# Keys' differences in the slot of x, k, v and rows in one gap, and weighted sums copied by ScalarE in one step a block

## The chip, the cores and the metric

The kernel runs on one core of a Trainium2 chip. The metric is the device time of one execution in microseconds (us). A core has a matrix engine (TensorE, PE in the profile), a vector engine (VectorE, DVE), an activation engine (ScalarE, ACT), a general engine (GpSimd, POOL), and SyncE (SP), which here only issues DMA transfers. Each works through its own queue in order. Matmul results land in PSUM[...]; everything else is in SBUF.

## The reference, cut to what matters

Two layers over x of shape (2, 256, 64, 64), all in fp32. The change touches only the first, attention with 8 heads of 32 channels over 4096 positions:

```
q, k, v = split(w_qkv @ x[b])                    # per image b, 8 heads, 32 x 4096 each
scores  = q.T @ k / sqrt(32)                     # 4096 x 4096 a head
attn    = softmax(scores, axis=-1)
x       = w_proj @ (attn @ v) + x
```

The second layer is a non-local block: three 1x1 convolutions, two of them followed by 2x2 max pooling, a softmax over 1024 keys, one more convolution, batch normalization and a residual.

## The kernel before, in words

**Groups and blocks.** Four heads of 32 channels fill 128 partitions, so a group n (0 to 3) is one image and four heads; two groups belong to an image. In a group a block i (0 to 7) is 512 queries, and in a block a step j (0 to 31) is 128 keys. `attend` (from line 410) holds the loops; after an image's two groups come `project` and `non_local`.

**A step.** For two pairs of heads, heads 2 and 3 first, TensorE makes scores into a `ps_s` tile (`score`, line 439), ScalarE takes the exponential into `p` (line 574), and a step later TensorE multiplies `p` with v into a PSUM tile `w` (`weigh`, line 463), which VectorE adds to the block's sum `blk.num`, a part of `y` (line 473). The scores of step 0 stand in PSUM together with the negated row maxima ("rows"); later steps add to them the product of q with a *difference* of keys, so that `s` is turned from one set of 128 keys to the next. The differences are tiles made by GpSimd: `kd` and `last_kd` (a chunk of 512 keys with an odd number less the one before it), `mid_kd` (even less odd) and `turn_kd`.

**The sums of p** are GpSimd's: it adds the first half's `p` (line 491) in each step, and in each second step issues a DMA that accumulates the other half (line 497). `normalize` finishes a block during the next one: a DMA and an add (`whole`, lines 506 and 510), a sum over partitions on TensorE (`den`, line 518), a reciprocal that goes out and back by DMA on SP, and a multiply on GpSimd (line 549). It is advanced at j = 1 and 5 and from j = 8 on.

**The maxima.** Before a block's softmax its row maxima over all keys are needed. They are computed ahead: `maxima(n, i)` is a generator that `attend` advances twice a step, four steps (LEAD) ahead of the block boundary, so the maxima of a block are made during the block before, and end in the step of j = 27 to 28. Each advance issues the matmuls of two heads (`product`, line 286). For heads 0 and 1 each of 8 chunks of keys is *plain*: one matmul, and one maximum reduction on VectorE (line 298). For heads 2 and 3 two chunks make a *pair*: q times the difference of the chunks, whose positive part ScalarE writes to a tile `over` (line 305); then q times the first chunk, and VectorE's one instruction adds `over` and reduces (line 312). In the first block of groups 1 to 3 only chunks 0 to 3 of heads 2 and 3 are pairs and 4 to 7 are plain (line 352): their differences would be in `last_kd`, which the group before still reads then. Head 3 starts with one plain chunk and ends with another. At the end VectorE reduces `part` to `neg` (line 380), GpSimd splits it (lines 141 to 145), and `make_rows` lets TensorE transpose it and ScalarE store it as rows.

**PSUM.** The pool `ps_m` has four banks, taken in turn by the maxima's `ps`, by `w`, `den`, the rows' `pt`, and by the products of `make`. A matmul waits until the tile that had its bank four allocations earlier is read. In a step that order is heads 0 and 1, heads 2 and 3, `w`.

**The next group's k, v and q** are made meanwhile: `make` (line 168) loads 512 columns of x over SP into the one slot of tag "x", multiplies, and lets ScalarE copy the product out. `during(n, i)` (line 267) lists three such items a block; they run at j = 11, 19 and 27. k's chunk 3 also brings two differences into `kd`. `renew` (line 250) has GpSimd make the other differences over again at the end of a group and the start of the next, behind the add of that step.

**Order.** The engines' queues are planned in the program's order with each instruction's readiness; `issue_after(x)` puts instructions behind x on its engine. A tile's buffer is taken again when all that read it is done: two buffers of `over`, five double and six single buffers for `p`.

Of the kernel before, what the change touches and what calls it, by code (L numbers as in the profile page):

```python
# [9 lines left out]
F32 = mybir.dt.float32  # L10
# [12 lines left out]
P = 128  # L23
NC = C // P
NB = 512
NI = N // NB
NJ = N // P
# [8 lines left out]
def conv_attention(  # L36
# [13 lines left out]
    nc = tc.nc  # L50
# [5 lines left out]
    xs = ctx.enter_context(tc.tile_pool(name="xs", bufs=1))  # L56
    qkv = ctx.enter_context(tc.tile_pool(name="qkv", bufs=2))
    work = ctx.enter_context(tc.tile_pool(name="work", bufs=2))
# [9 lines left out]
    def scores(name):  # L68
        return ps_s.tile([P, 2, NB], F32, tag="s", name=name)

    def scratch(name):
        return ps_m.tile([P, NB], F32, tag="m", name=name)
# [3 lines left out]
    def single(name):  # L76
        return probs.tile([P, 2, NB], F32, tag="one", name=name, bufs=ONES)

    def double(name):
        return probs.tile([P, 2, 2, NB], F32, tag="two", name=name, bufs=TWOS)  # L80
# [53 lines left out]
    t = const.tile([P, NB // P, QH, D], BF16, name="terms")  # L134
# [29 lines left out]
    QUAD = [(b, qd) for b in range(B) for qd in range(QUADS)]  # L164
    q, k, v, kd = {}, {}, {}, {}
    held = {}
# [61 lines left out]
    last_kd = const.tile([P, NI // 4, NB], F32, name="last_kd")  # L228

    def differences(n, c, to):  # L230
        two = k[n][:, bass.ts(c, 2 * NB)]
        nc.gpsimd.tensor_sub(to, two[:, NB:], two[:, :NB])  # L232
# [31 lines left out]

    def during(n, i):
        if i < NI - 2:
            return [("q", n, i + 2), ("k", n + 1, i), ("v", n + 1, i)]
        if i == NI - 2:  # L270
            return [("k", n + 1, i), ("k", n + 1, i + 1), ("q", n + 1, 0)]
        return [("v", n + 1, i - 1), ("v", n + 1, i), ("q", n + 1, 1)]


    reduced, cut = None, None
# [3 lines left out]
    LEAST = -3.4028234663852886e38  # L279
    part = const.tile([P, NB // P, QH, NI], F32, name="part")  # L280
    nc.vector.memset(part, LEAST)

    def product(n, i, g, h, keys, ps=None):
        if ps is None:
            ps = scratch(f"ps_{n}_{i}_{g}_{h}")
        nc.tensor.matmul(  # L286
            ps,
            q[n, i][bass.ts(h, D), bass.ts(g, P)],
            keys[bass.ts(h, D), :],
            start=True,  # L290
            stop=True,
        )
        return ps

    def plain(n, i, g, h, j):
        nonlocal reduced
        ps = product(n, i, g, h, k[n][:, bass.ts(j, NB)])
        reduced = nc.vector.tensor_reduce(part[:, g, h, j : j + 1], ps, AX.X, ALU.max)  # L298

    def pair(n, i, g, h, jp):  # L300

        nonlocal cut
        ps = product(n, i, g, h, (kd[n] if jp < NI // 4 else last_kd)[:, jp % (NI // 4), :])
        over = work.tile([P, NB], F32, tag="over", name=f"over_{n}_{i}_{g}_{h}")
        cut = nc.scalar.activation(over, ps, AF.Relu)  # L305
        yield
        joint(product(n, i, g, h, k[n][:, bass.ts(2 * jp, NB)]), over, g, h, jp)
        yield

    def joint(ps, over, g, h, jp):  # L310
        nonlocal reduced
        reduced = nc.vector.tensor_tensor_reduce(  # L312
            out=ps,
            in0=ps,
            in1=over,
            scale=1.0,
            scalar=LEAST,
            op0=ALU.add,
            op1=ALU.max,
            accum_out=part[:, g, h, 2 * jp : 2 * jp + 1],  # L320
        )
# [26 lines left out]
    def of_head(n, i, h):  # L348

        chunks = 0 if h < 2 else NI // 2 if i == 0 and n > 0 else NI
        pairs = [(g, jp) for jp in range(chunks // 2) for g in range(G)]
        plains = [(g, j) for g in range(G) for j in range(chunks, NI)]
        if h == 3:
            if not plains:
                g, jp = pairs.pop()
                plains = [(g, 2 * jp), (g, 2 * jp + 1)]
            plain(n, i, plains[0][0], h, plains[0][1])
            plains = plains[1:]  # L360
            yield
        for x in pairs:
            yield from pair(n, i, x[0], h, x[1])
        for x in plains:
            plain(n, i, x[0], h, x[1])
            yield

    def maxima(n, i):
        if (n, i) == (0, 0):
            yield from first_block()  # L370
        else:
            heads = [of_head(n, i, h) for h in range(QH)]
            for step in range(G * NI):

                for two in (0, 1), ((2, 3) if step % 2 == 0 else (3, 2)):
                    for h in two:
                        next(heads[h])
                    yield
        neg = work.tile([P, NB // P, QH], F32, tag="neg", name=f"neg_{n}_{i}")
        nc.vector.tensor_reduce(neg, part, AX.X, ALU.max, negate=True)  # L380
        rows.append(negate(f"{n}_{i}", neg))
        if i == 0 and n > 0:
            nc.vector.memset(part[:, :, 2:, :], LEAST)


    rows = []
# [8 lines left out]
    def advance(steps, n=1):  # L395
        for _ in range(n):
            next(steps, None)
# [12 lines left out]
    def attend(b, y):  # L410
# [11 lines left out]
        def keys(j):  # L422

            return j % NI * (NB // P) + j // NI
# [23 lines left out]
        def subtract(s, pair, blk):  # L448
            for t in range(2):
                h = 2 * pair + t  # L450
                nc.tensor.matmul(
                    s[:, t, :],
                    ones_b[bass.ts(h, D), :],
                    rows[blk.rows][bass.ts(h, D), :],
                    start=True,
                    stop=False,
                )

        def weigh(blk, j, p):

            w = scratch(f"w_{blk.name}_{j}")
            for h in range(QH):
                nc.tensor.matmul(  # L463
                    w[bass.ts(h, D), :],
                    v[blk.n][:, keys(j), h, :],
                    p[h // 2][:, h % 2, :],
                    start=True,
                    stop=True,
                )
            if j == 0:  # L470
                nc.vector.tensor_copy(blk.num, w)
            else:
                nc.vector.tensor_add(blk.num, blk.num, w)  # L473

# [3 lines left out]
        added = None  # L478
# [73 lines left out]
        for qd in range(QUADS):  # L552
            for i in range(NI):
                blk = Block(qd, i)
                items = [x for x in during(blk.n, i) if x[1] < len(QUAD)]
                both = [None, None]
                for j in range(NJ):
                    if j % 2 == 0:
                        two = double(f"p_{blk.name}_{j}_1")
                    p = [single(f"p_{blk.name}_{j}_0"), two[:, j % 2]]  # L560
                    for pair in (1, 0):
                        if j == 0:
                            s = both[pair] = scores(f"s_{blk.name}_{j}_{pair}")
                            subtract(s, pair, blk)
                            advance(maxes)
                            score(s, pair, blk, j)
                        else:
                            s = both[pair]
                            score(s, pair, blk, j)
                            advance(maxes)  # L570
                        with ExitStack() as order:
                            if cut is not None:
                                order.enter_context(tc.issue_after(cut.ins))
                            nc.scalar.activation(p[pair], s, AF.Exp, scale=scale)  # L574
                    if waiting is not None:
                        weigh(*waiting)
                        if j == 0:
                            normal = normalize(waiting[0])
                    add(blk, j, p, two)
                    waiting = blk, j, p  # L580
                    if j in (1, 5) or j >= AFTER:
                        advance(normal)
                    if j % 2 == 0:
                        make_rows()
                        if i > 0 and blk.n + 1 < len(QUAD) or i == 0 and blk.n > 0:
                            with tc.issue_after(added.ins) if added else ExitStack():
                                renew(i, j, blk.n)
                    elif j % 8 == 3 and j > 8 and items:
                        advance(make(*items.pop(0)), 9)
        weigh(*waiting)  # L590
        return normalize(blk)

# [205 lines left out]
    LEAD = 4  # L798
# [4 lines left out]
    items = [("k", 0), ("q", 0), ("k", 1), ("v", 0), ("q", 1), ("v", 1)]  # L803
# [76 lines left out]
```

## Time and profile before

| what | value |
|---|---|
| median of 3 runs | 3923.11 us (3920.67 to 3923.43) |
| profiled execution | 3922.51 us, its span 3920.7 us |
| TensorE matmul busy | 3882.0 us, 99% |
| VectorE busy | 2940.4 us, 75% |
| ScalarE busy | 2654.9 us, 68% |
| GpSimd busy | 3051.9 us, 78% |
| clock granted to TensorE | 0.997 |

Busy time is the time in which at least one instruction of the engine was under way. Matmuls overlap, so 99% says that TensorE always has one in flight, not that it couldn't do more. Row groups give a line, engine, operation and tiles, then how many, the busy time, the mean duration of one in ns, the idle time before them and what ended it. A timeline row starts with its start and duration in us; "x2" means that two instructions of a kind that follow each other are drawn together. Attention takes the stretches of about 106 to 1741 us and 2034 to 3630 us; the rest is `project` and `non_local`.

### The profile page before, as it was taken

To read this page: it belongs to the slowest core of one execution; us is meant where nothing else is said; L and a number is where in the kernel's file an instruction comes from. 1 tells how busy PE (TensorE), PEld (TensorE's weight loads), DVE (VectorE), ACT (ScalarE), POOL (GpSimd) and SP (SyncE) were. 2 spreads that over 40 slices of the span, in tenths; PEclk is the share of its full clock that TensorE was granted. 3 is DMA by queue.
4 is the path that set the end of the run, shared out by engine and by line. 5 is a ranking of instruction groups with operands and counts; after the bars stand their busy time and mean duration, and the time that the engine had idled before them with its cause. 6 is when DMAs were issued, how large, how long until landed. Compare 5 with 4: busy or idle time off the path is not lost.

```text
span 3920.7 us, 69957 instructions
## 1 busy us (share of the span) xinstructions
PE 3882.0 (99%) x27452; PEld 1370.0 (35%) x27452; DVE 2940.4 (75%) x5483; ACT 2654.9 (68%) x3296; POOL 3051.9 (78%) x1926
## 2 busy tenths in 40 slices
PE   8999999999999999999999999999999999999998
PEld 3333333333333333343333333333433333332333
DVE  5888888888888888874458888888888888885444
ACT  4777777777777777741137777777677787787011
POOL 1788888889888888871448889898899999997043
PEclk9999999999999999999999999999999999999999
DMA  1688888887888888880018888888888888889100
GB/s 57 139 168 169 167 170 168 174 169 167 166 167 169 165 169 169 172 195 6 22 38 167 167 173 170 170 171 175 165 173 169 169 170 168 167 167 188 54 16 27
DMA packets 113931, 569.40 MB, mean 145 GB/s; under 512 B 20296, under 2 KB 22600, under 8 KB 52416
## 3 DMA queue, kind: packets, MB, share of 16 engines
q0 software_dynamic: 68832, 501.25, 63.7%
q1 hardware_dynamic: 44080, 62.88, 4.6%
q8 instruction: 215, 3.52, 0.4%
q14 instruction: 116, 0.95, 0.1%
q10 hardware_dynamic: 688, 0.79, 0.1%
HBM read 54.78 MB, written 8.88 MB: 16 GB/s over the span
## 4 chain that ended last, share of the span: by engine, by line
PE 53%; DVE 2%; DMA 1%; ACT 0%; issue 0%; POOL 0%; DVEq 0%; ACTq 0%; POOLq 0%
PE s L439 14%; PE w L463 13%; PE ps L286 11%; PE y L736 6%; PE g L661 1%; DVE r L750 1%; PE f L704 1%; PE proj L604 1%; PE f L770 1%; PE q L198 1%; PE den L518 1%; PE tp L645 0%; PE tp L641 0%; PE v L186 0%; PE k L198 0%; DMA x_res<-in_x_dram 0%
## 5 line engine op out<-in xcount | busy, mean ns | idle before, releaser
L491 POOL TENSOR_TENSOR p<-p,p 128x1024 f32<-128x1024 f32 x945 | 2350.5, 2487 | 363.4 <-ACT p L574 338.4
L574 ACT ACTIVATE p<-s 128x1024 f32<-128x1024 f32 x2048 | 2085.9, 1023 | 593.3 <-PE ps L286 528.5
L286 PE MATMUL ps<-k,q 32*128 32x512 f32 x6232 | 2016.1, 627 | 4.0 <-DVE part L298 1.7
L298 DVE TENSOR_REDUCE part<-ps 128x1 f32<-128x512 f32 x2136 | 1369.0, 685 | 541.8 <-PE ps L286 541.6
L463 PE MATMUL w<-p,v 128*32 128x512 f32 x8192 | 1091.9, 605 | 0.6 <-ACT p L574 0.6
L439 PE MATMUL s<-q,mid_kd 32*128 32x512 f32 x3072 | 767.4, 615 | 0.0
L473 DVE TENSOR_TENSOR y<-y,w 128x512 f32<-128x512 f32 x992 | 679.1, 685 | 47.1 <-PE w L463 46.4
L312 DVE CUSTOM_DVE_ANT_0 ps<-ps,over 128x512 f32<-128x512 f32 x980 | 674.5, 691 | 34.3 <-PE ps L286 31.2
L286 PEld LDWEIGHTS ps<-k,q 32*128 32x128 f32 x6232 | 628.1, 183 | 43.3 <-DVE part L298 8.9
L305 ACT ACTIVATE over<-ps 128x512 f32<-128x512 f32 x916 | 541.9, 592 | 18.0 <-PE ps L286 12.6
L286 PE MATMUL ps<-kd,q 32*128 32x512 f32 x1056 | 517.0, 594 | 0.7 <-POOL kd L232 0.7
L439 PE MATMUL s<-q,kd 32*128 32x512 f32 x2048 | 512.2, 615 | 0.4 <-ACT p L574 0.3
L439 PE MATMUL s<-q,last_kd 32*128 32x512 f32 x2048 | 509.8, 614 | 0.7 <-ACT p L574 0.7
L463 PEld LDWEIGHTS w<-p,v 128*32 128x32 f32 x8192 | 161.1, 108 | 804.6 <-DVE part L298 775.0
L286 PE MATMUL ps<-last_kd,q 32*128 32x512 f32 x904 | 438.0, 593 | 2.4 <-POOL last_kd L232 2.4
L439 PEld LDWEIGHTS s<-q,mid_kd 32*128 32x128 f32 x3072 | 262.0, 183 | 413.9 <-ACT over L305 225.6
L497 POOL DMA_DIRECT2D p<-p x448 | 392.2, 875 | 4.4 <-issue 3.1
L439 PEld LDWEIGHTS s<-q,kd 32*128 32x128 f32 x2048 | 177.1, 183 | 295.4 <-ACT over L305 171.9
L439 PEld LDWEIGHTS s<-q,last_kd 32*128 32x128 f32 x2048 | 176.7, 183 | 275.8 <-ACT over L305 162.7
L736 PE MATMUL y<-p,kv 128*128 128x512 f32 x512 | 240.0, 608 | 6.4 <-DVE r L750 6.4
L785 ACT ACTIVATE p<-f 128x1024 f32<-128x1024 f32 x64 | 65.5, 1024 | 248.5 <-PE f L770 219.2
L732 POOL TENSOR_TENSOR sums<-sums,p 128x512 f32<-128x512 f32 x96 | 121.3, 1264 | 113.7 <-ACT p L785 109.9
(113 smaller groups left out, 2686.7 us busy)
## 6 DMA issues: line engine op xcount, KB each, us to landing
p<-p POOLq DMA_DIRECT2D x478, 1024.0 KB, 7.5
x_k<-in_x_dram SPq DMA_DIRECT2D x32, 512.0 KB
x_q<-in_x_dram SPq DMA_DIRECT2D x30, 512.0 KB
x_res<-in_x_dram SPq DMA_DIRECT2D x16, 512.0 KB
out_dram<-z SPq DMA_DIRECT2D x16, 512.0 KB
r<-flat SPq DMA_DIRECT2D x120, 64.0 KB
x_v<-in_x_dram SPq DMA_DIRECT2D x6, 512.0 KB
wqk_sb<-in_wqk_dram ACTq DMA_DIRECT2D x1, 512.0 KB
```

Of the source, the lines that this page charges most:

```text
L286: nc.tensor.matmul(ps, q[n, i][bass.ts(h, D), bass.ts(g, P)], keys[bass.ts(h, D), :], start=True, stop=True,)
L298: reduced = nc.vector.tensor_reduce(part[:, g, h, j : j + 1], ps, AX.X, ALU.max)
L305: cut = nc.scalar.activation(over, ps, AF.Relu)
L312: reduced = nc.vector.tensor_tensor_reduce(out=ps, in0=ps, in1=over, scale=1.0, scalar=LEAST, op0=ALU.add, op1=ALU.max, accum_out=part[:, ...
L439: nc.tensor.matmul(s[:, t, :], kj[bass.ts(h, D), :], q[blk.n, blk.i][bass.ts(h, D), :], start=False, stop=True, skip_group_check=j > 0,)
L463: nc.tensor.matmul(w[bass.ts(h, D), :], v[blk.n][:, keys(j), h, :], p[h // 2][:, h % 2, :], start=True, stop=True,)
L473: nc.vector.tensor_add(blk.num, blk.num, w)
L491: added = nc.gpsimd.tensor_add(blk.sums[0], blk.sums[0], p[0])
L497: sent = nc.gpsimd.dma_start(out=blk.sums[n], in_=two, accum_op=ALU.add)
L574: nc.scalar.activation(p[pair], s, AF.Exp, scale=scale)
L732: nc.gpsimd.tensor_add(acc[i][NC], acc[i][NC], p[:, j, :])
L736: nc.tensor.matmul(acc[i][o], wg[:, 2 * t + j, bass.ts(o, P)], p[:, j, :], **edge)
```

## The change

Three things are edited.

1. *Differences in the slot of x.* At j = 8 of a group's last block, GpSimd writes the differences of the next group's chunks 5 less 4 and 7 less 6 into a tile `first_kd` in the one "x" slot (`before_all`). In the first block of groups 1 to 3 `pair` reads them in place of `last_kd`, so all 8 chunks of heads 2 and 3 are pairs there, and the memset that reset `part` after that block goes.
2. *Places of the items.* `during` now gives the items by step: q at j = 11, k and v together at j = 30, the step in which rows are made. In block 6 k and v of chunk 6 come at j = 11, q of the next group's block 0 at j = 19 and k and v of chunk 7 at j = 30; in block 7 only q of the next group's block 1, at j = 7.
3. *A copy by ScalarE.* In one step a block, j = 26 (its `w` is weighed in the pass of j = 27), ScalarE copies `w` to a tile of tag "over" in SBUF and VectorE adds that to `blk.num`. The very last block is left out.

```diff
+    first_kd = {}
+
     def during(n, i):
         if i < NI - 2:
-            return [("q", n, i + 2), ("k", n + 1, i), ("v", n + 1, i)]
+            return {11: [("q", n, i + 2)], NJ - 2: [("k", n + 1, i), ("v", n + 1, i)]}
         if i == NI - 2:
-            return [("k", n + 1, i), ("k", n + 1, i + 1), ("q", n + 1, 0)]
-        return [("v", n + 1, i - 1), ("v", n + 1, i), ("q", n + 1, 1)]
+            return {
+                11: [("k", n + 1, i), ("v", n + 1, i)],
+                19: [("q", n + 1, 0)],
+                NJ - 2: [("k", n + 1, i + 1), ("v", n + 1, i + 1)],
+            }
+        return {7: [("q", n + 1, 1)]}
+
+    def before_all(n):
+        held.clear()
+        first_kd[n] = xs.tile([P, NI // 4, NB], F32, tag="x", name=f"first_kd_{n}")
+        for c in range(2):
+            differences(n, NI // 4 + c, first_kd[n][:, c, :])
...
-        ps = product(n, i, g, h, (kd[n] if jp < NI // 4 else last_kd)[:, jp % (NI // 4), :])
+        those = kd[n] if jp < NI // 4 else first_kd[n] if i == 0 and n > 0 else last_kd
+        ps = product(n, i, g, h, those[:, jp % (NI // 4), :])
...
-        chunks = 0 if h < 2 else NI // 2 if i == 0 and n > 0 else NI
+        chunks = 0 if h < 2 else NI
...
-        if i == 0 and n > 0:
-            nc.vector.memset(part[:, :, 2:, :], LEAST)
...
+            elif j == NJ - LEAD - 2 and (blk.n, blk.i) != (len(QUAD) - 1, NI - 1):
+                t = work.tile([P, NB], F32, tag="over", name=f"w_{blk.name}")
+                nc.scalar.copy(t, w)
+                nc.vector.tensor_add(blk.num, blk.num, t)
             else:
                 nc.vector.tensor_add(blk.num, blk.num, w)
...
-                items = [x for x in during(blk.n, i) if x[1] < len(QUAD)]
+                items = during(blk.n, i)
...
-                    elif j % 8 == 3 and j > 8 and items:
-                        advance(make(*items.pop(0)), 9)
+                        if (i, j) == (NI - 1, 8) and blk.n + 1 < len(QUAD):
+                            with tc.issue_after(added.ins):
+                                before_all(blk.n + 1)
+                    for item in items.get(j, ()):
+                        if item[1] < len(QUAD):
+                            advance(make(*item), 9)
```

## The prediction

> **What bounds the kernel now.** I read the page first (busy times, the chain), then stretches of one block, then the timeline at two places. The page:
>
> ```profile
> PE 3882.0 (99%) x27452; PEld 1370.0 (35%) x27452; DVE 2940.4 (75%) x5483; ACT 2654.9 (68%) x3296; POOL 3051.9 (78%) x1926
> ...
> PE 53%; DVE 2%; DMA 1%; ACT 0%; issue 0%; POOL 0%; DVEq 0%; ACTq 0%; POOLq 0%
> ...
> L473 DVE TENSOR_TENSOR y<-y,w 128x512 f32<-128x512 f32 x992 | 679.1, 685 | 47.1 <-PE w L463 46.4
> ```
>
> TensorE carries the chain. A step is the time from one start of `w` (line 463) to the next: 2.96 us nearly everywhere, six waves of four matmuls (0.43 apart, 0.13 more at each change between row tiles and column tiles). Extra work shows as a longer step: q or k +1.91, v +1.98, `den` +0.86, rows +0.33, first scores +0.17. Three whole blocks (ordinary; last of four heads; ordinary of the last four heads):
>
> ```profile
> 614.40:716.20 101.80, 101.80 (x812) 34.92 (x808) 83.08 (x163) 80.01 (x101) 90.29 (x53) 1.00 0.81 169
> 818.80:925.40 106.60, 106.60 (x824) 42.27 (x828) 90.22 (x164) 73.73 (x86) 94.02 (x57) 1.00 0.76 159
> 2956.00:3054.90 98.90, 98.90 (x792) 32.97 (x796) 83.16 (x163) 79.02 (x99) 90.49 (x53) 1.00 0.82 169
> ```
>
> The columns are length, then PE, PEld, DVE, ACT, POOL. An ordinary block adds up: 32 x 2.96 + 0.86 + 1.91 (q) + 1.91 (k) + 1.98 (v's step) + 0.33 + 0.17 = 101.9. POOL is at 90 to 94: a step with its add and half a DMA issue takes about 2.83 of 2.96, so it only catches up where TensorE has extra work.
>
> The place of the copy is the step from j = 27 to 28, where one block's maxima end. Without v in it (last four heads) it takes 3.90, 0.94 over. TensorE, then VectorE, there:
>
> ```profile
> 3134.55 1.06 PE L463 MATMUL w<-p,v 128*32 128x512 f32 x8
> ...
> 3137.40 1.12 PE L286 MATMUL ps<-k,q 32*128 32x512 f32 x2
> 3138.45 1.06 PE L463 MATMUL w<-p,v 128*32 128x512 f32 x8
> ```
>
> ```profile
> 3136.46 0.29 DVE L380 TENSOR_REDUCE neg<-part 128x16 f32<-128x128 f32 x1
> 3136.66 0.68 DVE L473 TENSOR_TENSOR y<-y,w 128x512 f32<-128x512 f32 x1
> 3137.26 1.99 DVE L298 TENSOR_REDUCE part<-ps 128x1 f32<-128x512 f32 x3
> ```
>
> A third plain reduction and `neg` make VectorE late; the `y` add that frees the bank of `w` ends at 3137.34, and the matmul that wants the bank starts at 3137.40, alone, two waves (0.86) after its partners. That is the 0.94. POOL meanwhile:
>
> ```profile
> 3135.70 0.84 POOL L497 DMA_DIRECT2D p<-p  x1
> 3136.30 2.62 POOL L491 TENSOR_TENSOR p<-p,p 128x1024 f32<-128x1024 f32 x1
> ```
>
> [...] The one VectorE add of that kind is line 489, in the last block (its 15 durations are min, median, max), with VectorE and then POOL around two of them:
>
> ```profile
> L489 DVE TENSOR_TENSOR p<-p,p x15: 1218/1226/4104, 3551.1 to 3625.5; 128x1024 f32<-128x1024 f32 x15
> ```
>
> ```profile
> 3551.11 4.10 DVE L489 TENSOR_TENSOR p<-p,p 128x1024 f32<-128x1024 f32 x1
> ...
> 3562.59 1.56 DVE L489 TENSOR_TENSOR p<-p,p 128x1024 f32<-128x1024 f32 x1
> ```
>
> ```profile
> 3551.47 5.97 POOL L491 TENSOR_TENSOR p<-p,p 128x1024 f32<-128x1024 f32 x2
> ...
> 3560.70 2.36 POOL L491 TENSOR_TENSOR p<-p,p 128x1024 f32<-128x1024 f32 x1
> ```
>
> The second starts 0.47 before POOL's add ends (3563.06) and ends 1.09 after it, so it ran only then; the first, started even a little before POOL's, took 4.10 in place of 1.23. The adds of line 473, whose `w` is in PSUM, stay at 0.69 beside the same POOL adds. [...]
>
> **The change part by part.** Sums are for the profiled execution: span 3920.7, 3922.51 with what lies around it, 0.6 under the median.
>
> *Pairs for plains* in the block before the second to fourth group of four heads. Before, that block is 106.58: 32 x 2.96 + 0.86 + v 1.98 + v 1.98 + q in the closing step 2.61 + 0.33 + 0.17 = 102.65, so 3.93 is VectorE's, in steps of 3.45 with four reductions and the `y` add. All other blocks have the same 16 pairs a head and run at 2.96, so all of it goes: 3 x 3.93 = 11.8 (bounds 0 and 11.8). ScalarE gets 16 more Relus of 0.592 in that block, 9.5 over 73.7 busy of about 101, in the place that they have in every block.
> The price is on POOL: two differences of 1.37, three times, queued at j = 8 behind the add; behind them stand the adds, DMA issues and, at j = 26 to 30, the renewed differences. POOL's work in that block becomes about 94 + 2.7 = 97, on a block that falls to about 98 to 101. What is late next is `whole` in the next block, and with it a buffer of p: in the last group's first block ScalarE already waits 2.3 for it and the step is 5.03 in place of 3.82. I take 2 for all three places (0 to 8; 5 where no other stall lets POOL catch up). The memset that goes (0.11, three times) is beside TensorE's work.
>
> *k, v and rows in one gap.* Before, per group: 6 q at 1.91 and 2 in the closing step at 2.61 + 8 k at 1.91 + 6 v at 1.98 in the closing step + 2 v at 1.98 + 8 rows at 0.33 = 50.4. Those in the closing step include its 0.94, which v and q covered. After: 8 q 15.3; seven gaps of rows 0.33 + k 1.71 + v 1.79 + 0.2 for one entry and exit = 4.03, 28.2; k and v alone 3.7; rows alone 0.3; sum 47.5. So 2.9 less per group, but each closing step now costs its stall e on its own: 2.9 - 8e. Three groups: 8.8 - 24e. If nothing is shared in the gap it is 0.2 more each, 4 in all. The ScalarE copies (0.59 each) fall into the gap. x loads on SP: k and v share one, the six `x_v` loads go; the shortest time ahead stays 8 steps, 24 us, and the waits list no TensorE wait for x in attention. They stand behind the `r` transfers of j = 14, long issued. The kd differences go from j = 19 to j = 30 with k, and POOL has 4 us there. All at nothing.
>
> *The copy.* It adds 31 ScalarE copies at 0.59 ([...] the copies of line 212 show 592). ScalarE is idle for 1.00 just there, so at 3136.31 the bank is free, the late matmul runs with its partners, and of the 0.94 only VectorE's order remains. But the add now has both inputs in SBUF. It is ready at about 3136.4, `neg` ends at 3136.75[...]. The add then ends 0.55 after that (0.69 less the 0.14 that the longer add saved), 3139.47; the reduction behind it on VectorE ends at 3140.1, and it frees the bank that the next `w` waits for: 3140.16 in place of 3137.51, so e = 2.65. POOL stands at the same phase in nearly every block. Bounds: e = 0 if the add comes behind the reductions and still hides, [...] 3.2 if it falls behind one more POOL instruction. I take 2.65: the trace's own case started before POOL's and lost. In the last group, blocks 0 to 5 go from 0.94 to e: 6 x (0.94 - e); block 6 has no maxima behind it, 0.
>
> Sum with e = 2.65: -11.8 + 2 - 8.8 + 24 x 2.65 + 6 x 1.71 = +55. Span 3976, with the 1.8 around it 3977.5, on the median's scale 3978. The likeliest case's own range is 3955 to 3992 (e from 2 to 3.2).
>
> **Rivals.**
> 1. [...] comes after the reductions and waits 0.3: e about 0.6. Sum -11.8 + 5 - 8.8 + 14.4 - 2.0 = -3: 3920. [...] Against: case 3551.11.
> 2. *The other side, faster: VectorE's two reductions go ahead of the add and its wait is taken up in the idle 0.39 of each step*, e = 0.1: -11.8 + 5 - 8.8 + 2.4 - 5.0 = -18: 3905. It decides at e = 0.4, where the sum passes -8. Against: the profile has the `y` add ahead of the reductions.
> 3. *POOL becomes the bound at the group ends*: rival 1 with 8 to 15 more, 3931. For: 2.3 already waited. Against: only two of the three places run on into attention.
> That the plains don't vanish is in none of them; it would cost 11.8.
>
> **How the numbers follow.** Forecast 0.56, rival 1 0.18, rival 2 0.20, rival 3 0.06. 0.2%, 8 us, is about what a measurement of this kernel can tell. Slower takes the forecast and two thirds of rival 3: 0.60. Same takes 0.12 of rival 1 and the rest of rival 3: 0.14. Faster takes rival 2 and 0.06 of rival 1: 0.26. The range 3908 to 3992 leaves out most of rival 2 (0.15) and 0.05 above.
>
> **What would show it.** Right: `y` adds with two SBUF inputs, 31 of them, far over 0.69 (about 2.7), ending 0.55 after a POOL add; closing steps of 5.6; gaps at j = 30 of about 7.0; last blocks of a group without 3.45 steps. Wrong: these adds at 0.69, or closing steps under 3.6. A gap well over 7.0, or first blocks with stalls over 2 at j = 6 to 8, would put the loss elsewhere.

## The result and the profile after

The changed kernel takes 4047.31 us (median of 4 runs, 4045.61 to 4047.57) against 3921.89 us before (4 runs, 3919.51 to 3923.43): a ratio of 1.0318, 95% interval 1.0305 to 1.0331. It is slower, as forecast, but by 125 us in place of 55.

The page of the changed kernel: busy times, then the chain, then two of the costliest groups (line, engine, operation, tiles, count, busy time, mean ns of one, idle time before them and what ended it).

```profile
PE 3913.3 (97%) x27452; PEld 1369.8 (34%) x27452; DVE 3003.0 (74%) x5480; ACT 2694.6 (67%) x3372; POOL 3069.9 (76%) x1932
...
PE 49%; DVE 3%; issue 2%; DMA 1%; POOL 0%; ACT 0%; DVEq 0%; POOLq 0%; ACTq 0%
...
L474 PE MATMUL w<-p,v 128*32 128x512 f32 x8192 | 1111.7, 615 | 91.1 <-DVE part L311 90.5
...
L490 DVE TENSOR_TENSOR y<-y,w 128x512 f32<-128x512 f32 x961 | 658.4, 685 | 76.5 <-PE w L474 75.3
```

TensorE's share falls from 99% to 97%, and the reason stands in the third row: before the `w` matmuls it now waits 90.5 us for VectorE's plain maximum reduction (line 311). Such a wait wasn't in the list before. But 90.5 is less than 125, and TensorE's busy time has grown by 31.3 us (3882.0 to 3913.3) with the same 27452 matmuls: some of them have become slower.

The answer for VectorE's instructions on `y` (count; duration as min, median and max in ns; first and last start):

```profile
L490 DVE TENSOR_TENSOR y<-y,w x961: 626/686/690, 110.0 to 3754.1; 128x512 f32<-128x512 f32 x193
...
L488 DVE TENSOR_TENSOR y<-y,w x31: 681/4021/4099, 186.8 to 3653.7; 128x512 f32<-128x512 f32 x31
```

The 961 adds that read `w` from PSUM stay at 0.69 us. The 31 that read its copy (line 488) have a median of 4.02.

The three blocks of the kind shown before (length; PE, PEld, DVE, ACT, POOL busy; granted clock; DMA share; GB/s):

```profile
641.10:748.10 107.00, 103.38 (x815) 35.60 (x811) 86.41 (x163) 80.71 (x102) 90.79 (x53) 0.98 0.77 161
859.80:959.10 99.30, 98.27 (x792) 32.81 (x795) 83.90 (x163) 79.56 (x100) 93.76 (x57) 1.00 0.77 158
3054.10:3157.50 103.40, 99.78 (x792) 33.06 (x788) 86.47 (x163) 79.66 (x100) 90.85 (x53) 0.98 0.77 160
```

An ordinary block went from 101.80 to 107.00, and in it TensorE is now idle for 3.62 and its mean clock is 0.98. The last block of four heads went the other way, 106.60 to 99.30: it lost its steps of 3.45 and two of its three items. The third kind went from 98.90 to 103.40.

The waits of TensorE have one new line (us in total, times, longest):

```profile
PE w L474 <- DVE part L311: 90.5, 30, 3.6
```

And this is one such wait, in the closing step of a block in the last four heads: TensorE, VectorE, GpSimd and ScalarE in turn, each row with start and duration.

```profile
3237.23 1.06 PE L474 MATMUL w<-p,v 128*32 128x512 f32 x8
...
3244.02 1.94 PE L474 MATMUL w<-p,v 128*32 128x512 f32 x8 [3.62 <-DVE part L311]
...
3249.61 1.31 PE L474 MATMUL w<-p,v 128*32 128x512 f32 x8
```

```profile
3239.14 0.29 DVE L393 TENSOR_REDUCE neg<-part 128x16 f32<-128x128 f32 x1
3239.35 4.02 DVE L488 TENSOR_TENSOR y<-y,w 128x512 f32<-128x512 f32 x1
3243.29 1.88 DVE L311 TENSOR_REDUCE part<-ps 128x1 f32<-128x512 f32 x3
```

```profile
3238.96 2.63 POOL L508 TENSOR_TENSOR p<-p,p 128x1024 f32<-128x1024 f32 x1
3241.26 1.54 POOL L566 TENSOR_TENSOR y<-y,r 128x512 f32<-128x512 f32 x1
3242.47 0.99 POOL L141 CAST terms<-neg 128x16 bf16<-128x16 f32 x1
```

```profile
3238.36 0.58 ACT L487 COPY w<-w 128x512 f32<-128x512 f32 x1
```

ScalarE's copy is done at 3238.94. The add starts at 3239.35, as soon as `neg` lets it, and ends at 3243.37: 0.57 after GpSimd's multiply (ends 3242.80), not 0.57 after GpSimd's add of `p` (ends 3241.59). It stood behind both. The reduction behind it frees the bank, and the next `w` starts at 3244.02: a closing step of 6.79 in place of 3.90. The step after it takes 5.59 in place of 2.96, though nothing waits in it. The stretches around it say why (columns as above):

```profile
3237.00:3240.00 3.00, 3.00 (x28) 1.45 (x24) 2.89 (x7) 2.55 (x4) 3.00 (x3) 1.00 0.76 158
3240.00:3243.00 3.00, 0.41 (x4) 0.00 (x0) 3.00 (x1) 1.94 (x3) 3.00 (x3) 1.00 1.03 213
3243.00:3246.00 3.00, 1.98 (x12) 0.32 (x12) 2.16 (x4) 0.00 (x0) 2.71 (x6) 0.56 0.47 96
3246.00:3250.00 4.00, 4.00 (x20) 1.31 (x24) 2.05 (x4) 1.25 (x2) 1.63 (x2) 0.50 0.00 0
3250.00:3253.00 3.00, 3.00 (x28) 0.97 (x24) 2.29 (x5) 2.25 (x4) 1.77 (x2) 0.97 0.87 175
```

From 3243.34 on, still in the gap of 3.62, the granted clock is half for 6.83 us, in which four matmuls start about every 0.85 us and not every 0.43. That is the second part of the loss. In attention the record of the kernel before holds one such stretch, of 6.83 us from 2030.7 on, which reaches into the first step of the second image; that of the changed kernel holds 26 (14 of 3.41 us, 12 of 6.83), 129.7 us in all. Of these, 25 belong to closing steps and one to the last block.

The changed kernel also has the milder case. In blocks 0 and 16 (of 32, counted through all four groups), each the first of an image, no multiply follows GpSimd's add of `p`: VectorE's add takes 2.88 and 2.89, the closing steps 5.58 and 5.59, and TensorE is idle for 2.41.

**Where the time went.** From the starts of the `w` matmuls come all the steps' times. This is their excess over 2.958 us, in us, summed over the blocks 0 to 29, for the profiled executions of both kernels and of four kernels told of below.

| steps | before | after | no_copy | copy_no_add | mul_later | pool_add |
|---|---|---|---|---|---|---|
| closing, j = 27 to 28 | 57.0 | 97.0 | 28.0 | 4.4 | 69.3 | 4.6 |
| the one after it | 0.0 | 51.1 | 0.0 | 0.0 | 37.6 | 3.2 |
| rows, with k and v after the change | 9.9 | 84.6 | 84.6 | 84.6 | 84.6 | 84.6 |
| j = 11 | 57.7 | 57.1 | 57.1 | 57.1 | 57.1 | 57.1 |
| j = 19 | 46.2 | 5.8 | 5.7 | 5.7 | 5.7 | 5.7 |
| j = 7 and 8 | 25.3 | 31.5 | 31.3 | 31.6 | 31.5 | 31.5 |
| plain chunks, last blocks | 11.9 | 0.1 | 0.1 | 0.0 | 0.1 | 0.0 |
| first six | 1.7 | 5.5 | 5.3 | 6.4 | 3.4 | 7.4 |

Before, v or q ran in 24 of these 30 closing steps and covered their stall; no_copy shows the stall bare, 28.0 for all 30. The changed kernel's first two rows are 120 us above no_copy's; the two profiled executions differ by 123.

### The profile page after: what moved, and what is told of

The parts are those of the page before. It is cut to its first block, busy times and chain, and to the rows that moved or that the text cites. A ratio compares the mean times of both kernels' runs of the same rounds, so it can differ in the third digit from the quotient of the medians.

```text
span 4045.7 us, 70021 instructions
## 1 busy us (share of the span) xinstructions
PE 3913.3 (97%) x27452; PEld 1369.8 (34%) x27452; DVE 3003.0 (74%) x5480; ACT 2694.6 (67%) x3372; POOL 3069.9 (76%) x1932
## 4 chain that ended last, share of the span: by engine, by line
PE 49%; DVE 3%; issue 2%; DMA 1%; POOL 0%; ACT 0%; DVEq 0%; POOLq 0%; ACTq 0%
PE s L450 13%; PE w L474 12%; PE ps L299 10%; PE y L757 5%; PE proj L625 1%; PE g L682 1%; DVE r L771 1%; PE f L725 1%; PE f L791 1%; DVE part L311 1%; DMA p<-p 1%; PE q L198 1%; PE den L535 0%; PE tp L666 0%; PE tp L662 0%
## 5 line engine op out<-in xcount | busy, mean ns | idle before, releaser
L299 PE MATMUL ps<-k,q 32*128 32x512 f32 x6142 | 2039.2, 637 | 4.0 <-DVE part L311 1.7
L311 DVE TENSOR_REDUCE part<-ps 128x1 f32<-128x512 f32 x2046 | 1315.1, 685 | 578.9 <-PE ps L299 578.8
L474 PE MATMUL w<-p,v 128*32 128x512 f32 x8192 | 1111.7, 615 | 91.1 <-DVE part L311 90.5
L326 DVE CUSTOM_DVE_ANT_0 ps<-ps,over 128x512 f32<-128x512 f32 x1025 | 706.6, 692 | 40.6 <-PE ps L299 29.9
L490 DVE TENSOR_TENSOR y<-y,w 128x512 f32<-128x512 f32 x961 | 658.4, 685 | 76.5 <-PE w L474 75.3
L319 ACT ACTIVATE over<-ps 128x512 f32<-128x512 f32 x961 | 569.3, 592 | 27.1 <-PE ps L299 15.4
L450 PE MATMUL s<-q,last_kd 32*128 32x512 f32 x2048 | 542.5, 651 | 5.7 <-ACT p L591 5.7
L299 PE MATMUL ps<-kd,q 32*128 32x512 f32 x1056 | 530.9, 608 | 0.7 <-POOL kd L232 0.7
L450 PEld LDWEIGHTS s<-q,mid_kd 32*128 32x128 f32 x3072 | 270.2, 183 | 442.8 <-ACT over L319 257.6
```

Of the source, the lines that this page charges most:

```text
L299: nc.tensor.matmul(ps, q[n, i][bass.ts(h, D), bass.ts(g, P)], keys[bass.ts(h, D), :], start=True, stop=True,)
L326: reduced = nc.vector.tensor_tensor_reduce(out=ps, in0=ps, in1=over, scale=1.0, scalar=LEAST, op0=ALU.add, op1=ALU.max, accum_out=part[:, ...
L450: nc.tensor.matmul(s[:, t, :], kj[bass.ts(h, D), :], q[blk.n, blk.i][bass.ts(h, D), :], start=False, stop=True, skip_group_check=j > 0,)
L474: nc.tensor.matmul(w[bass.ts(h, D), :], v[blk.n][:, keys(j), h, :], p[h // 2][:, h % 2, :], start=True, stop=True,)
```

## The experiments

**Theories.** A: the copy costs the time, since its add waits for GpSimd; one part of the loss is the wait itself (behind one GpSimd instruction or two), the other the halved clock after TensorE's idle time. B, the rival: the new places of k and v, or the longer POOL queue with the new differences, cost a good part of it. Theory A was tested by taking out the copy, its add, and the second GpSimd instruction in turn, and by moving the add to GpSimd; B by making the moves alone.

**no_copy: the changed kernel without the copy.** VectorE adds `w` from PSUM in every step.

```diff
-            elif j == NJ - LEAD - 2 and (blk.n, blk.i) != (len(QUAD) - 1, NI - 1):
-                t = work.tile([P, NB], F32, tag="over", name=f"w_{blk.name}")
-                nc.scalar.copy(t, w)
-                nc.vector.tensor_add(blk.num, blk.num, t)
             else:
                 nc.vector.tensor_add(blk.num, blk.num, w)
```

> The changed kernel with VectorE adding w from PSUM in all steps; k, v and rows in one gap and the pairs stay. Theory (the loss is the add's wait for POOL, and the slow clock behind it): the closing steps fall from 6.8 to 3.90 and the steps after them from 4.6-5.6 to 2.96, so 149 us go and 30 x 0.94 come back: about 3926 us. Rival (the gap of k, v and rows, or the copies' buffers, cost the time): it stays above 4000 us.

Measured: 3924.49 (12 runs) beside 3922.82 before, ratio 1.0004 (0.9996 to 1.0013). The closing step is 3.90 and the one after it 2.96. So the other two edits together cost nothing that can be told from no change, and on top of them the copy costs the whole loss. What it costs without them is told under copy_only.

**copy_no_add: the copy without its add.** ScalarE still copies, and VectorE leaves that one term of 32 out of each block's sum (not of the last block's).

```diff
                 nc.scalar.copy(t, w)
-                nc.vector.tensor_add(blk.num, blk.num, t)
```

> The changed kernel with ScalarE's copy kept and the add of that copy left out, so the term of one step a block is missing from the weighted sums. Theory: ScalarE's copy costs nothing and frees the bank, so the closing step is 3.1 or less and the next one 2.96: about 3903 us. Rival (the copy delays ScalarE, or its over buffer holds up a Relu): closing steps of 4 or more remain, above 4000 us.

Measured: 3901.16 (3 runs), ratio 0.9950 (0.9934 to 0.9966). The closing step is 3.10, no later step is long. The copy on ScalarE by itself costs TensorE nothing; it takes 0.8 off each closing step, because the bank of `w` comes free early. What costs is the add.

**mul_later: GpSimd's multiply two steps later**, so that a cast to `terms` and not the multiply stands behind GpSimd's add in the closing step.

```diff
-                for _ in range(13):
+                for _ in range(15):
                     yield
```

> The changed kernel with GpSimd's multiply of the normalization at j = 29 in place of 27, so that it doesn't stand right behind the add of p that VectorE's add meets. Theory (VectorE waits through two GpSimd instructions, 4.02 us, and TensorE idle for 3.6 us gets half the clock): VectorE's add takes about 2.8, TensorE is idle for 2.4, the step after keeps the full clock; e falls from 5.0 to 2.65 a block, about 3977 us. Were the clock not tied to the length of the idle stretch, the next step would stay 1.6 longer: about 4022 us. Were the multiply not what it waits for: 4047 us.

Measured: 4002.52 (2 runs), ratio 1.0203 (1.0183 to 1.0224). Its adds of the copies, its wait for VectorE, and a stretch of the step after a closing one (clock in the third column from the end):

```profile
L488 DVE TENSOR_TENSOR y<-y,w x31: 680/2820/2885, 187.0 to 3609.3; 128x512 f32<-128x512 f32 x31
```

```profile
PE w L474 <- DVE part L311: 62.8, 30, 2.4
```

```profile
3205.00:3210.00 5.00, 4.09 (x24) 1.38 (x24) 3.10 (x6) 0.49 (x2) 3.56 (x6) 0.66 0.51 105
```

The add takes 2.82 in place of 4.02, and the closing step 5.59 in place of 6.79: exactly the second instruction, 1.2. These are the closing steps of the prediction. But the clock still falls: TensorE's idle time of 2.4 is enough in 23 of 25 such steps, now nearly always for 3.41 us, and the step after takes 4.61. That an idle time of 3.6 is needed, the author's estimate on which the expectation of 3977 rested, fell.

Why two steps of 25 escape can be read from the records. In each record all stretches of half clock start on one grid of 3.413 us (the 27 here to within 0.01 us). Where the idle time of 2.4 lies in one interval of that grid, or 2.22 of it do, the half clock follows, 23 times; the two that escape, blocks 0 and 24, are the two that a grid line cuts into 0.78 and 1.63, and 0.74 and 1.60.

**pool_add: GpSimd adds the copy**, ahead of its add of `p`; the split of `neg` is put behind it.

```diff
...
-        rows.append(negate(f"{n}_{i}", neg))
+        with tc.issue_after(late.ins) if late else ExitStack():
+            rows.append(negate(f"{n}_{i}", neg))
...
                 nc.scalar.copy(t, w)
-                nc.vector.tensor_add(blk.num, blk.num, t)
+                blk.copied = late = nc.gpsimd.tensor_add(blk.num, blk.num, t)
...
             elif j < NJ - 1:
-                added = nc.gpsimd.tensor_add(blk.sums[0], blk.sums[0], p[0])
+                with tc.issue_after(blk.copied.ins) if blk.copied else ExitStack():
+                    added = nc.gpsimd.tensor_add(blk.sums[0], blk.sums[0], p[0])
```

> The changed kernel with the copied sum added by GpSimd (1.27 us for 128 x 512), ahead of its add of p in that step, in place of VectorE; the split of neg queues behind it. Theory: no VectorE instruction with two SBUF inputs is left in the block, the closing step falls to about 3.1: about 3906 us, below the kernel before. Rival (GpSimd is so full that 31 more instructions bind): more stalls at the group ends and at the block starts, 3925 us or more.

Measured: 3910.05 (7 runs), ratio 0.9968 (0.9957 to 0.9980), so 0.3% faster than the kernel before, and 137 us faster than the changed one. GpSimd's add of the copy:

```profile
L491 POOL TENSOR_TENSOR y<-y,w x31: 1477/1488/1577, 186.5 to 3515.2; 128x512 f32<-128x512 f32 x31
```

It takes 1.48 to 1.58 every time (the 1.27 expected is the median of line 241's differences of the same shape before); VectorE no longer adds two SBUF tiles in these steps. Closing steps fall to 3.11 and the first two rows of the table from 148 to 7.8. It is 9 us, 0.2%, above copy_no_add, with 1.49 more on GpSimd a block; 3.2 of the 9 stands in the step after and 1.0 in the first six, and the rest isn't assigned.

**copy_only: the kernel before with the copy alone.**

```diff
                 nc.vector.tensor_copy(blk.num, w)
+            elif j == NJ - LEAD - 2 and (blk.n, blk.i) != (len(QUAD) - 1, NI - 1):
+                t = work.tile([P, NB], F32, tag="over", name=f"w_{blk.name}")
+                nc.scalar.copy(t, w)
+                nc.vector.tensor_add(blk.num, blk.num, t)
             else:
```

> The kernel before with the one step's copy by ScalarE and VectorE's add of the copy, nothing else; v (or q) still runs in the closing step. Theory: VectorE's add waits 4.0 us as in the changed kernel, so that the step lasts 6.8 in place of 4.94 (v), 5.57 (q) or 3.90 (nothing): 18 x 1.85 + 6 x 1.2 + 6 x 2.9 = 58 us. TensorE works on v for 1.8 of the wait and is idle for less than 2, so the slow clock follows in the six blocks without v alone, 6 x 2.1 = 13: about 3994 us. Were the slow clock to follow in all blocks: about 4030 us. Rival (the gap of k, v and rows is needed for the loss): within 10 us of the kernel before.

Measured: 3991.89 (4 runs) beside 3923.17, ratio 1.0174 (1.0157 to 1.0191). VectorE's adds of the copies, and one of them beside GpSimd:

```profile
L477 DVE TENSOR_TENSOR y<-y,w x31: 681/4033/4644, 188.5 to 3599.0; 128x512 f32<-128x512 f32 x31
```

```profile
917.51 4.64 DVE L477 TENSOR_TENSOR y<-y,w 128x512 f32<-128x512 f32 x1
```

```profile
917.74 2.63 POOL L497 TENSOR_TENSOR p<-p,p 128x1024 f32<-128x1024 f32 x1
920.05 1.55 POOL L555 TENSOR_TENSOR y<-y,r 128x512 f32<-128x512 f32 x1
```

The adds wait as long as in the changed kernel, and most closing steps are 6.8 as well. But in 24 of 30 blocks v or q is made in that step, which gives TensorE 1.9 us of other work and leaves it idle for at most 1.83 (1.45 at 922.81, in the block of the rows above). There the clock stays full (2 of 24 blocks excepted, both with 1.83 idle). In the six blocks of the last four heads, which have no v, TensorE idles for 3.62 and the step after takes 4.56 or 5.59, six times of six. So the copy alone costs 69 us on the kernel before, and 123 on the kernel with the moves and the pairs. The move of v out of the closing step is what bares the copy's wait and lets it bring the clock down in every group.

**gap_only: the kernel before with the items at their new places.**

```diff
-            return [("q", n, i + 2), ("k", n + 1, i), ("v", n + 1, i)]
+            return {11: [("q", n, i + 2)], NJ - 2: [("k", n + 1, i), ("v", n + 1, i)]}
...
-                    elif j % 8 == 3 and j > 8 and items:
-                        advance(make(*items.pop(0)), 9)
+                    for item in items.get(j, ()):
+                        if item[1] < len(QUAD):
+                            advance(make(*item), 9)
```

> The kernel before with the items at their new places, nothing else: the plain chunks and the copy stay as before. Theory: 3.9 a gap and k and v together save 3 to 4 a group of four heads, each closing step shows its own 0.94: -11 + 24 x 0.94 = +11 us: about 3934 us, 10 above the changed kernel without the copy, which has the pairs in addition. Rival (the pairs gain nothing because GpSimd gives it back): as that one, 3924 us.

Measured: 3933.07 (11 runs) beside 3923.17, ratio 1.0025 (1.0016 to 1.0034): 10 slower, and the closing steps of 3.90 stand bare, since v no longer hides their stall of 0.94. Between no_copy and gap_only stand the pairs: 1.0004 less 1.0025 is about -8 us. Places and pairs together thus come to nothing: B costs nothing by itself. Its one share in the loss is that of copy_only, the wait that v would have covered.

**early_add: the add ahead of `neg`.** In the changed kernel VectorE reduces `neg` behind the add of the copy, so the add starts 0.33 earlier against GpSimd.

```diff
...
-        nc.vector.tensor_reduce(neg, part, AX.X, ALU.max, negate=True)
+        with tc.issue_after(late.ins) if late else ExitStack():
+            nc.vector.tensor_reduce(neg, part, AX.X, ALU.max, negate=True)
...
-                nc.vector.tensor_add(blk.num, blk.num, t)
+                late = nc.vector.tensor_add(blk.num, blk.num, t)
```

> The changed kernel with one order edit: VectorE reduces neg behind the add of the copy, not ahead of it, so that the add comes 0.33 us earlier, into the 0.86 us in which GpSimd issues a DMA and does not yet read. Theory (the add waits only if GpSimd's read is under way): it takes 0.7, the closing step about 3.45, nothing follows: 30 x 4.5 less than the changed kernel, about 3912 us. [...] still about 4045 us.

Measured: 4063.03 (4 runs) beside 3922.48, ratio 1.0360 (1.0341 to 1.0378), where an add that still waits was put at about 4045. VectorE and GpSimd in one closing step:

```profile
617.04 4.38 DVE L490 TENSOR_TENSOR y<-y,w 128x512 f32<-128x512 f32 x1
621.35 0.27 DVE L394 TENSOR_REDUCE neg<-part 128x16 f32<-128x128 f32 x1
```

```profile
617.03 2.62 POOL L510 TENSOR_TENSOR p<-p,p 128x1024 f32<-128x1024 f32 x1
619.35 1.52 POOL L568 TENSOR_TENSOR y<-y,r 128x512 f32<-128x512 f32 x1
```

The add starts in the same hundredth as GpSimd's and still loses; it ends at 621.42, again 0.55 after the multiply. Starting earlier only makes it wait longer, and `neg` behind it comes late: closing steps of 7.18. The theory that the add waits only for a read that is already under way fell. In the changed kernel itself the add was served at once in a few blocks. One of them:

```profile
1693.89 0.68 DVE L488 TENSOR_TENSOR y<-y,w 128x512 f32<-128x512 f32 x1
```

```profile
1693.74 0.86 POOL L514 DMA_DIRECT2D p<-p  x1
1694.35 2.67 POOL L508 TENSOR_TENSOR p<-p,p 128x1024 f32<-128x1024 f32 x1
```

Here it starts 0.46 ahead of GpSimd's record, during the DMA issue, and wins. At 0.23 ahead (copy_only, 917.51) it lost. The lead alone doesn't decide it, though. In the last block of the kernel before, VectorE's own add of `p` at 3551.11 started 0.36 ahead and lost (4.10), and another went first with less lead:

```profile
3580.65 1.22 DVE L489 TENSOR_TENSOR p<-p,p 128x1024 f32<-128x1024 f32 x1
```

```profile
3580.97 3.13 POOL L491 TENSOR_TENSOR p<-p,p 128x1024 f32<-128x1024 f32 x1 [2.05 <-ACT p L574]
```

It started 0.32 ahead and took its usual 1.22; GpSimd's add took 3.13 in place of 2.36. What decides the records don't show.

## Why the prediction was right in kind and wrong in size

**Where the loss comes from: right.** The add with two SBUF inputs waits for GpSimd: it takes 4.02 us beside GpSimd's add and multiply and ends 0.55 to 0.57 after the second, and the 961 adds whose `w` is in PSUM take 0.69. Before the run this was the author's estimate, from the adds of two SBUF tiles in line 489 of the kernel before (4.10 and 1.56 beside GpSimd's add, median 1.23). That the new add takes 0.69 where nothing holds it up was not shown then; the shortest of the 31 took 0.68. No_copy and copy_no_add show that this add turns a version of 3924 (added from PSUM) or 3901 (not added at all) into 4047. Its direction, too, was as forecast.

**What failed: the term e of the copy**, in "The add then ends 0.55 after that ... so e = 2.65" (after the end of GpSimd's add, 3138.92), and its upper bound of 3.2. Over 30 closing steps the sum had 79.5 us; the first two rows of the table have 148.0, 4.93 each. The 68.5 between are nearly the whole miss of 69 (4047 against 3978). They have two causes.

1. *Two GpSimd instructions, not one: 17.5 us.* "It falls behind one more POOL instruction" was the bound, not the value taken, and it had that case at 3.2. It is worth 1.2 more: 2.65 + 1.2 = 3.85, and the closing steps of 6.79 have 3.83. The 17.5 is the net of 23 steps with two instructions, 27 over, and five in which the add was served early, 10 under. The multiply stood in the trace before, right behind the add of `p` that the prediction priced:

```profile
3138.62 1.52 POOL L549 TENSOR_TENSOR y<-y,r 128x512 f32<-128x512 f32 x1
```

It ends at 3140.14, 1.22 after that add, so the bound was too low by the prediction's own kind of working. Mul_later takes that instruction away, and the closing step is 5.59 where the prediction had 5.6.
2. *The clock: 51.1 us.* The prediction treated a stall as lost time alone and put the clock at nothing. TensorE idles for 3.62 in it, its clock halves for 3.41 or 6.83 us, and the step behind takes 4.6 or 5.6. Less idle time does it too: 2.4 us in 23 of 25 such steps (mul_later). The trace before had a sign of it, just ahead of attention: a wait of TensorE of 1.69, then half clock for 10.24 us from 92.0 on (clock third from the end of the second row).

```profile
90.48 1.13 PE L286 MATMUL ps<-k,q 32*128 32x512 f32 x4 [1.69 <-DVE part L298]
```

```profile
92.00:96.00 4.00, 4.00 (x15) 1.59 (x12) 1.68 (x4) 1.18 (x2) 0.00 (x0) 0.50 0.00 0
```

The prediction showed the clock of whole blocks alone, which was 1.00. Its own stall of 2.65, of which about 2.4 is idle, was longer than that wait.

**The rest of the sum held.** Pairs for plains: forecast -11.8, measured 11.9 to 0.1. Their price on GpSimd: 2 forecast; the first six steps went from 1.7 to 5.5, but gap_only, without the pairs, has 3.1 there, so about 2.2 (no_copy's 5.3 less 3.1) is theirs. The gap of k, v and rows: forecast a step 4.03 over, measured 6.85, 3.89 over; k and v alone 3.70 in both. All moves together, with a closing stall of 0.94: forecast -8.8 + 24 x 0.94 = 13.8; rows two to six of the table and the closing one, no_copy less before, give 10.6, and gap_only 10.

**The rivals.** Rival 1, an add that doesn't wait for GpSimd's, is what happens in a few blocks (0.68), not in the others; early_add shows that it isn't a matter of 0.33 us. Rival 2, the add's wait hides, fell: 4.02 us can't hide in an idle 0.39. Rival 3, GpSimd as the bound at the group ends, has its 2 to 4 us and no more. The sign by which the forecast was to be known, adds of "about 2.7", stood at 4.02; "closing steps of 5.6" at 6.79.

**What is left open.** Why VectorE isn't served between GpSimd's add and its multiply, while in mul_later it is between the add and a cast (2.82), and in the last block of the kernel before it was between two adds of `p` (4.10 for an add of 1.23, behind one). There the second add's record starts 0.08 after the first ends; the multiply's starts 0.33 before the add ends, but so does the cast's.

## What to carry to other kernels

A VectorE add whose second input moves from PSUM to SBUF can gain a wait behind GpSimd (here it went from 0.69 to 4.02 us), and that wait can take in more than one GpSimd instruction (here the add and the multiply, but not the cast behind them): read GpSimd's next two rows before pricing it, or give the add to GpSimd (3910 here, against 4047). Where a forecast stall leaves TensorE idle for as long as here (half clock followed 2.4 us in 23 of 25 steps of mul_later, and 3.6 us in all 23 of the changed kernel), add the price of its clock to the stall's own length (here 1.3 to 2.6 us a stall). Work that fills a stall, as v did here, is then worth more than its hidden time: beside it the clock also stayed full, in 22 of 24 blocks of copy_only.

## What the runs showed of the hardware

- In closing steps, an idle time of TensorE of 3.55 to 3.62 us was followed by half clock each time (23 times in the changed kernel, 6 in copy_only), for 3.41 or 6.83 us; of 2.4 us in 23 of 25 (mul_later), mostly for 3.41; of 1.83 in 2 of 15 (copy_only); of 1.45 or less never. Elsewhere less was enough at times: 1.69 before 92.0 in the kernel before, 1.49 before 938.6 in no_copy.
- All stretches of half clock of a record start on one grid of 3.413 us (29 in the changed kernel, to within 0.01 us), and how the idle time falls on it matters: 2.4 us cut by a grid line into 0.78 and 1.63 had no effect (mul_later), 2.41 cut into 0.50 and 1.91 was followed by half clock (the changed kernel, idle from 187.92 on).
- VectorE's [128, 512] fp32 add with two SBUF inputs waited for a GpSimd add whose record starts 0.23 us later (4.64, copy_only) and didn't where that starts 0.46 us later (0.68). With [128, 1024] adds it waited at 0.36 (4.10) and didn't at 0.32 (1.22, and GpSimd's add took 3.13). It wasn't held up by GpSimd's DMA issue (0.68 beside it). By the starts that the records give, the earlier one isn't always the one that goes first.
- The [128, 512] add was not served between two `tensor_tensor` instructions of GpSimd that follow each other at once, add and multiply, in any of the closing steps of 6.79 (4.02 us each); its end was 0.55 to 0.57 after the second.
- GpSimd's own add of the same shape took 1.48 to 1.58 us (pool_add).
